# Two buffers for the attention's scaled products, and the mask bounds as a ring of three half blocks

## The chip, the cores and the metric

The kernel runs on one core of a Trainium2 chip. The core has a matrix engine (TensorE, PE in the profile; its weight loads are listed apart as PEld), a vector engine (VectorE, DVE), a scalar engine (ScalarE, ACT), GpSimd (POOL) and SyncE (SP), which here only issues transfers and passes on semaphores. Matmul results go to PSUM, everything else lives in SBUF, and large arrays in HBM. The metric is the device time of one execution in microseconds, the median of several runs.

## The reference

Two graph layers work on x of shape (8, 2048, 256): eight batches of 2048 nodes with 256 features. The mask adj (2048 x 2048, zeros and ones) is common to all batches and to both layers.

```python
# layer 0: attention with 4 heads of 64; keys in 8 chunks of 256, each with a softmax of its own
h = relu(layernorm(x))
q, k, v = h @ Wq.T + bq, h @ Wk.T + bk, h @ Wv.T + bv        # split into heads
scores = clip(einsum('bhnd,bhjcd->bhnjc', q, kc) / 8, -10, 10)
scores = where(mask == 0, -10, scores)
attn = softmax(scores, axis=-1)                              # over the 256 keys of a chunk
ctx = einsum('bhnjc,bhjcd->bhnd', attn, vc)                  # summed over the chunks
out = layernorm(ctx @ Wo.T + bo + h) * gamma + beta
x = x + out
# layer 1: additive graph attention
h = relu(layernorm(x)); g = h @ W
e = leaky_relu(g @ a1 [:, :, None] + g @ a2 [:, None, :], 0.01)
e = where(adj == 0, -1e9, e)
x = x + relu(softmax(e) @ g)
```

Since every chunk has its own softmax, the context of a query is the sum over eight chunks of (exponentials times values) divided by that chunk's sum of exponentials.

## The kernel before

**The mask.** In the setup the mask is turned into *bounds*: one int8 per (key, query), large where the edge exists and -10 times the scale where it does not. A clip of the logits to the bounds (L530, VectorE) then does both the masking and the upper clip; layer 1 uses the same bounds with a comparison (L946, VectorE) that zeroes the weights of missing edges. The bounds of one block of 512 queries against all 2048 keys are 1 MB. There are four such blocks, kept in HBM as `bound_d`, and two of them fit in SBUF at a time (`bound_tile`, tag `bound`, two buffers). They are made from the adjacency in 32 parts, a part being 128 queries by half of the keys: VectorE compares (L277), GpSimd permutes half of the parts (L281), TensorE turns the part (L292), and ScalarE writes the bounds (L303), for the first two blocks straight into the SBUF tiles, for the other two into a small tile `bound_part` that GpSimd's queue (later ScalarE's) sends to HBM (L306). `store_bounds` sends the first two blocks to HBM at slot 2 of the first batch.

**Layer 0, per batch.** Attention runs in 32 steps n = (nb, j): four query blocks nb by eight key chunks j. The steps are software pipelined by hand. Iteration f has a first part `begin` and a second part `end`; at iteration f, step f-1 has its logits and clips, step f-2 its exponentials, its sums and half of its value products, step f-3 the other half of its value products and its scaling. Iteration f stands for the *slots* 2f and 2f+1, and a table `todo` hangs the other work of the batch (norms, output projection, loads, fetches) on slots. The order of instructions on every engine is the order in which the Python code issues them.

In a step TensorE makes the logits (L490), multiplies exponentials and values (L506, into two PSUM tiles `ps_n`) and sums the exponentials with ones (L518, from `both`, which GpSimd adds up in L545). These matmuls use quarters of the array, and a bank of PSUM is written by two of them in turn; a `fence` (L462), which is an empty instruction on SyncE's queue, keeps the two apart. SyncE's queue therefore carries transfers and fences in one order. ScalarE inverts the sums (L550, L551), VectorE multiplies the two `ps_n` by them (`scale`, L560), into `ctxT` for the first chunk of a block, and into a tile `prod` (one buffer) for the other seven. GpSimd's queue then adds prod to ctxT by an accumulating transfer (`gather`, L565). A later scaling writes prod again, so it waits until that transfer has landed. Value products of later steps need the `ps_n` tiles that the scaling frees.

**Layer 1, per batch.** 16 pieces (nb, j4), each of 512 queries by 512 keys. `weights` makes the masked weights on VectorE (L940, L946) two pieces ahead of `products` on TensorE (L963). A whole block of bounds serves four pieces, and a half block two. Meanwhile the batch after the next is loaded and normed (`far`), and the attention of the next batch is begun (`early`).

**When the bounds are fetched** (`fetch_bounds`, L174, SyncE's queue): attention's blocks 1, 2 and 3 at the slots 6 (not in the first batch), 20 and 36; layer 1's block 0 at slot 52 and block 1 at slot 66; layer 1's blocks 2 and 3 and the next batch's block 0 in layer 1's pieces 4, 8 and 12.

Of the kernel before, what the change touches and what calls it, by code (L numbers as in the profile page):

```python
# [8 lines left out]
F32 = mybir.dt.float32  # L9
BF16 = mybir.dt.bfloat16  # L10
I32 = mybir.dt.int32
I8 = mybir.dt.int8
AF = mybir.ActivationFunctionType
ALU = mybir.AluOpType
# [3 lines left out]
P = 128  # L18
# [10 lines left out]
def gnn_two_layers(  # L29
# [18 lines left out]
    nc = tc.nc  # L48
# [5 lines left out]
    NT = N // P  # L54
    NB = 512
    TB = NB // P
    NNB = N // NB
    NCH = N // CHUNK
    KT = CHUNK // P
# [4 lines left out]
    xpool = ctx.enter_context(tc.tile_pool(name="xpool", bufs=2))  # L64
# [29 lines left out]
    work = ctx.enter_context(tc.tile_pool(name="work", bufs=2, reuse_waits="tile"))  # L94
# [20 lines left out]
    bound_d = [kept.tile([P, NT, NB], I8, name=f"bound_d{nb}") for nb in range(NNB)]  # L115
    bounds, bounds1 = {}, {}
# [50 lines left out]
        return queries.rearrange("p (t i b) -> p t i b", i=QUADS, b=Q)  # L167

    def bound_tile():
        return xpool.tile([P, NT, NB], I8, tag="bound", name="bound", bufs=2)  # L170

    def fetch_bounds(nb):
        t = bound_tile()
        nc.sync.dma_start(t, bound_d[nb])  # L174
        return t

    def store_bounds(nb):
        nc.sync.dma_start(bound_d[nb], bounds[nb])


    lone = const.tile([P, NT], F32, name="lone")
# [32 lines left out]
    def pe(piece):  # L214

        piece.kind = "pe"
        return piece
# [40 lines left out]
    def load_rows(t, half):  # L258
        rows = xpool.tile([P, HALF], I32, tag="x", name="rows", bufs=NNB)
        of_block = adj[t // TB * NB:(t // TB + 1) * NB, half * HALF:(half + 1) * HALF]  # L260
        nc.sync.dma_start(rows, of_block.rearrange("(p t) k -> p t k", t=TB)[:, t % TB, :])
        return rows
# [32 lines left out]
    def keep_bounds(pt, t, half):  # L295

        nb, rows, cols = t // TB, slice(half * 8, (half + 1) * 8), slice((t % TB) * P, (t % TB + 1) * P)
        if nb in bounds:
            dst = bounds[nb][:, rows, cols]
        else:  # L300
            tag = part_tags[(2 * t + half) % 4] if in_setup[0] else "r"
            dst = work.tile([P, 8, P], I8, tag=tag, name="bound_part", bufs=2 if tag == "r" else 1)
        nc.scalar.activation(dst, pt, AF.Copy, scale=-2.0 * CLIP * SC, bias=CLIP * SC)  # L303
        if nb not in bounds:
            queue = nc.gpsimd if in_setup[0] else nc.scalar
            queue.dma_start(bound_d[nb][:, rows, cols], dst)  # L306

# [71 lines left out]
    class Projection:  # L379
# [40 lines left out]
        def fetch(self, nb):  # L420
            self.hT[nb] = Features(turned_d[0][nb])
# [47 lines left out]
    class Attention:  # L469
# [55 lines left out]
        def clip(self, n, o):  # L525
            nb, j = self.STEPS[n]
            p, i = self.ORDER[o]
            if (n, p) not in self.e:
                self.e[n, p] = work.tile([P, 2 * KT, NB], F32, tag="e", name="e", bufs=5)
            nc.vector.scalar_tensor_tensor(  # L530
                self.e[n, p][:, i * KT:(i + 1) * KT, :], self.s.pop((n, o)), -CLIP * SC,
                bounds[nb][:, j * KT:(j + 1) * KT, :], op0=ALU.max, op1=ALU.min,
            )

        def exponentials(self, n, o):
# [17 lines left out]
        def scale(self, n, c):  # L553
            nb, j = self.STEPS[n]
            if j == 0 and c == 0:
                self.ctxT[nb] = work.tile([P, 2, NB], F32, tag="ctx", name="ctxT")
            if j > 0 and c == 0:
                self.prod[n] = work.tile([P, 2, NB], F32, tag="prod", name="prod", bufs=1)
            dst = self.ctxT[nb] if j == 0 else self.prod[n]
            nc.vector.tensor_tensor(dst[:, c, :], self.num.pop((n, c)), self.rz[n], op=ALU.mult)  # L560

# [317 lines left out]
    class Layer1:  # L879
# [56 lines left out]
        def weights(self, nb, j4):  # L936
            w = work.tile([P, 4, NB], F32, tag="e", name="w", bufs=5)
            for i in range(4):
                j = 4 * j4 + i
                nc.vector.tensor_scalar(  # L940
                    w[:, i, :], self.src[nb], self.cd[:, 0, j:j + 1], self.cd[:, 1, j:j + 1],
                    op0=ALU.mult, op1=ALU.max,
                )
                if i % 2:
                    two = w[:, i - 1:i + 1, :]
                    nc.vector.scalar_tensor_tensor(  # L946
                        two, bounds1[nb][:, j - 1:j + 1, :], 0.0, two, op0=ALU.is_gt, op1=ALU.mult
                    )
            return w

# [49 lines left out]
    STEPS2 = 2 * STEPS  # L1000
    HALVES = STEPS2 + 6
    PER = STEPS2 // NNB
# [14 lines left out]
    rows = {i: load_rows(*nearest[i]) for i in range(4)}  # L1017
# [20 lines left out]
        for i in parts:  # L1038
            keep_bounds(turn_missing(found.pop(i)), *nearest[i])

    for nb in range(2):
        bounds[nb] = bound_tile()
    proj.stats(1, range(TB))
    proj.power(1)
    proj.shift(1)
# [1 line left out]
    for nb in range(NNB - 1):  # L1047
        i = 6 * nb
# [44 lines left out]
    def layer1_vector(i):  # L1093
# [9 lines left out]

    once = {
        1: [lambda: raws.update(o=load_output_weight(wo)), layer1_weight],
        2: [lambda: store_bounds(0), lambda: store_bounds(1)],
        5: [pe(lambda: turn_weight(raws["o"], woT))],
        6: [lambda: layer1_vector(0)],
        7: [lambda: layer1_vector(1)],
# [8 lines left out]
    for b in range(B):  # L1118
# [4 lines left out]
        ahead = projs.get(b + 1)  # L1123
# [5 lines left out]
        def at(n, *pieces):  # L1129
            todo.setdefault(n, []).extend(pieces)  # L1130
# [4 lines left out]
        def early(i):  # L1135
            one.products(accs[0], ws.pop(i), i)

        def fetch(of, nb):
            of[nb] = fetch_bounds(nb)

        for nb in range(NNB - 1):
            for n, pieces in blocks[nb].beside().items():
# [1 line left out]
        if b == 0:  # L1144
            for n, pieces in once.items():
                at(n, *pieces)

            beats = [(12, 13, 18, 19), (31, 32, 33, 34), (44, 46, 47, 48), (57, 58, 59, 60)]
            for nb, ns in enumerate(beats):
                at(ns[0] - 5, lambda nb=nb: ahead.load(nb))  # L1150
                for t, n in enumerate(ns):
                    at(n, lambda nb=nb, t=t: ahead.stats(nb, [t]))
                n = ns[-1]
                at(n + 1, lambda nb=nb: ahead.power(nb))
                at(n + 2, lambda nb=nb: ahead.shift(nb))
                at(n + 3, lambda nb=nb: ahead.norm(nb, 0))
                at(n + 4, lambda nb=nb: ahead.norm(nb, 1))
                at(n + 4, lambda nb=nb: ahead.flip(nb, 0))
                at(n + 5, lambda nb=nb: ahead.flip(nb, 1))
                at(n + 7, lambda nb=nb: ahead.send(nb))  # L1160
        else:
            at(6, lambda: fetch(bounds, 1))
        at(PER + 4, lambda: fetch(bounds, 2))
        at(2 * PER + 4, lambda: fetch(bounds, 3))
        at(3 * PER + 4, lambda: fetch(bounds1, 0))
        at(STEPS2 + 2, lambda: fetch(bounds1, 1))
        at(STEPS2 - 6, last.load)
        at(STEPS2, lambda: last.residual(0))

# [98 lines left out]
        else:  # L1268
# [33 lines left out]
            last.power1()  # L1302
            last.shift1()
            weights(2)
            last.norm1(0)
            last.norm1(1)
            early(1)
# [9 lines left out]
            one.send(3)  # L1317
            one.receive(2)
            weights(4)

        far = projs[b + 2] = Projection(b + 2) if b + 2 < B else None
        if far:
            far.adder = nc.gpsimd
        for i, (nb, j4) in enumerate(pieces1):
            if not ahead and i < 3:
                continue
            if i + 2 < len(pieces1):
                weights(i + 2)
            if nb not in accs:
                accs[nb] = one.accumulators(nb)  # L1330
            if j4 == 1 and nb + 1 < NNB:
                one.received(nb + 1)
                if nb + 2 < NNB:
                    one.receive(nb + 2)
            if j4 == 2:
                one.alone(nb)
            one.products(accs[nb], ws.pop(i), j4)
            if j4 == 0 and nb > 0:
                one.finish(nb - 1, accs[nb - 1])
            if j4 == 0 and nb > 0 and nb + 1 < NNB:  # L1340
                fetch(bounds1, nb + 1)
            if ahead and (nb, j4) == (NNB - 1, 0):
                fetch(bounds, 0)
            if j4 == 1 and nb > 0:
                one.store(nb - 1)
            if far and i in (3, 6, 9, 12):
                far.send(i // 3 - 1)
            if far and i in (0, 3, 6, 9):
                far.load(i // 3)
            if far and i in (1, 4, 7, 10):  # L1350
                far.stats(i // 3, range(TB))
                far.power(i // 3)
                far.shift(i // 3)
            if far and i in (2, 5, 8, 11):
                for t2 in range(2):
                    far.norm(i // 3, t2)
                for t2 in range(2):
                    far.flip(i // 3, t2)
            if ahead and i == len(pieces1) - 4:
                att = Attention(ahead)  # L1360
            if ahead and i >= len(pieces1) - 4 and i < len(pieces1) - 1:
                att.early(i - (len(pieces1) - 4))
                if i == len(pieces1) - 2:
                    att.early(3)
# [34 lines left out]
```

## Time and profile before

| | us |
|---|---|
| median of 3 runs | 3558.47 (3555.39 to 3564.36) |
| profiled execution | 3563.89 |
| its span, first to last instruction | 3562.1 |
| TensorE busy | 3527.6 |
| VectorE busy | 2639.0 |
| ScalarE busy | 1947.4 |
| GpSimd busy | 1808.9 |
| first sums of exponentials (L518), end of setup | 88.2 |

The profile lists one execution. A busy time is the union of an engine's instructions; "idle before" is the time in which the engine stood still just ahead of an instruction, and the name behind it is what ended it. The ends of matmuls are modelled, so TensorE's busy share is no measure of its rate; the starts are recorded. The rows of SP and of queues (a q behind the engine) are issues of transfers and waits for semaphores, and are not counted as busy.

### The profile page before, as it was taken

Reading aid. Unit: us, or ns where it says so; the run is one execution under the profiler, and the core shown is the slowest. Engines: PE = TensorE matmul, PEld = TensorE weight load, DVE = VectorE, ACT = ScalarE, POOL = GpSimd, SP = SyncE. Lnnn points to the kernel's source line nnn. Section 1 sums busy time; section 2 is a strip of 40 time slices with the busy share of each in tenths; the row PEclk is TensorE's granted clock in tenths of the full one; section 3 lists DMA queues with packets and bytes.
Section 4 is the critical chain, followed back from the end, with each engine's and each line's share of the span. In section 5 each row is a group of like instructions: output and inputs, shape, how many; then the busy total and the mean of one; then the engine's idle time right before and its main releaser. Section 6 shows DMA issues by size and latency. Waiting matters only on the chain.

```text
span 3562.1 us, 104433 instructions
## 1 busy us (share of the span) xinstructions
PE 3527.6 (99%) x46080; PEld 2183.0 (61%) x46080; DVE 2639.0 (74%) x3979; ACT 1947.4 (55%) x2961; POOL 1808.9 (51%) x1182
## 2 busy tenths in 40 slices
PE   8999999999999999999999999999999999999999
PEld 5455785557755577555775557655586555855568
DVE  7888677867678676786767867678586785757866
ACT  6677426763267633676236762367624766147750
POOL 2688016870278702786037850378404784048731
PEclk9999999999999999999999999999999999999999
DMA  7545423444234441344423444234442434124321
GB/s 234 119 107 134 87 74 85 91 113 91 80 79 85 123 95 60 85 96 109 92 66 85 97 110 91 71 79 91 120 103 55 91 81 118 57 55 91 85 69 48
DMA packets 169111, 329.74 MB, mean 93 GB/s; under 512 B 35664, under 2 KB 97360, under 8 KB 160464
## 3 DMA queue, kind: packets, MB, share of 16 engines
q1 hardware_dynamic: 127696, 203.51, 19.2%
q0 software_dynamic: 32640, 118.50, 18.0%
q8 instruction: 360, 5.90, 0.7%
q10 hardware_dynamic: 8320, 1.05, 0.2%
q14 instruction: 95, 0.78, 0.1%
HBM read 154.14 MB, written 51.43 MB: 58 GB/s over the span
## 4 chain that ended last, share of the span: by engine, by line
PE 97%; DVE 1%; DMA 1%; ACT 1%; issue 0%; POOL 0%; ACTq 0%; DVEq 0%; POOLq 0%; SPq 0%
PE ps_s L490 25%; PE ps_n L506 24%; PE ps_s L963 12%; PE ps_t L518 7%; PE ps_n L963 6%; PE ps_t L963 6%; PE ps_t L714 2%; PE ps_t L434 2%; PE ps_n L434 2%; PE ps_s L434 2%; PE ps_t L814 2%; PE ps_n L814 2%; PE ps_t L448 1%; PE ps_n L448 1%; DVE z L277 0%
## 5 line engine op out<-in xcount | busy, mean ns | idle before, releaser
L530 DVE SCALAR_TENSOR_TENSOR e<-ps_s,bound 128x1024 f32<-128x1024 f32 x1024 | 1224.1, 1220 | 404.0 <-PE ps_s L490 400.6
L545 POOL TENSOR_TENSOR both<-e 128x1024 f32<-128x1024 f32 x512 | 1219.8, 2407 | 571.1 <-PE ps_t L518 355.6
L490 PE MATMUL ps_s<-q,k 64*32 64x512 f32 x16384 | 1431.8, 590 | 1.5 <-DVE e L530 1.4
L539 ACT ACTIVATE e<-e 128x1024 f32<-128x1024 f32 x1024 | 1050.6, 1050 | 481.1 <-DVE e L530 462.7
L506 PE MATMUL ps_n<-e,v 64*32 64x512 f32 x16384 | 1224.9, 591 | 2.4 <-DVE prod L560 2.4
L506 PEld LDWEIGHTS ps_n<-e,v 64*32 64x32 f32 x16384 | 460.9, 107 | 473.1 <-issue 384.1
L490 PEld LDWEIGHTS ps_s<-q,k 64*32 64x32 f32 x16384 | 459.5, 106 | 448.6 <-issue 331.2
L518 PE MATMUL ps_t<-both,ones 64*32 64x512 f32 x4096 | 537.9, 592 | 0.1
L963 PE MATMUL ps_s<-g,w 128*128 128x257 f32 x2048 | 447.8, 380 | 0.0
L963 PEld LDWEIGHTS ps_s<-g,w 128*128 128x128 f32 x2048 | 388.8, 190 | 56.3
L560 DVE TENSOR_TENSOR prod<-ps_n,rz 128x512 f32<-128x512 f32 x448 | 288.5, 686 | 162.8 <-PE ps_n L506 96.1
L986 POOL TENSOR_TENSOR x<-x,r 128x256 f32<-128x256 f32 x124 | 90.7, 745 | 466.2 <-ACT r L984 465.4
L946 DVE SCALAR_TENSOR_TENSOR w<-bound,w 128x1024 f32<-128x1024 int8 x256 | 314.7, 1229 | 8.7
L354 POOL TENSOR_TENSOR krn<-krn,mv 128x4 f32<-128x4 f32 x28 | 6.8, 242 | 575.4 <-DVE w L940 575.4
L963 PE MATMUL ps_n<-g,w 128*128 128x257 f32 x1024 | 292.4, 382 | 0.0
L963 PE MATMUL ps_t<-g,w 128*128 128x257 f32 x1024 | 289.7, 380 | 0.0
L550 ACT ACTIVATE rz<-ps_t 128x512 f32<-128x512 f32 x256 | 152.6, 596 | 229.4 <-PE ps_t L518 201.5
L940 DVE TENSOR_SCALAR w<-src,cd 128x512 f32<-128x512 f32 x512 | 263.1, 556 | 7.0 <-ACT src L921 6.6
L963 PEld LDWEIGHTS ps_n<-g,w 128*128 128x128 f32 x1024 | 192.8, 190 | 44.3 <-issue 17.6
L565 POOL DMA_DIRECT2D ctxT<-prod x224 | 191.0, 853 | 54.1 <-DVE prod L560 46.7
L963 PEld LDWEIGHTS ps_t<-g,w 128*128 128x128 f32 x1024 | 193.8, 189 | 28.2
L551 ACT ACTIVATE rz<-rz 128x512 f32<-128x512 f32 x256 | 161.4, 630 | 8.2
(133 smaller groups left out, 2910.4 us busy)
## 6 DMA issues: line engine op xcount, KB each, us to landing
ctxT<-prod POOLq DMA_DIRECT2D x224, 512.0 KB, 4.9
bound<-bound_d SPq DMA_DIRECT2D x62, 1024.0 KB, 6.2
turned_d<-squares SPq DMA_DIRECT2D x232, 128.0 KB, 2.4
hT<-turned_d SPq DMA_DIRECT2D x58, 512.0 KB, 4.3
rows<-in_adj_dram SPq DMA_DIRECT2D x32, 512.0 KB, 5.3
x<-in_x_dram SPq DMA_DIRECT2D x32, 512.0 KB, 4.9
out_dram<-x SPq DMA_DIRECT2D x31, 512.0 KB, 2.6
xp<-in_x_dram SPq DMA_DIRECT2D x28, 512.0 KB, 4.5
```

What stands on the lines that cost most here:

```text
L434: nc.tensor.matmul(in_key_order(pp) if i == 0 else pp, w[:, di, do * P:(do + 1) * P], h, start=di == 0, stop=di == FC - 1,)
L490: nc.tensor.matmul(self.s[n, o][c * Q:(c + 1) * Q, kt, :], self.k[p][rows, at:at + Q], self.q[p][rows, nb * NB:(nb + 1) * NB], start=True, ...
L506: made.append(nc.tensor.matmul(self.num[n, c][h * Q:(h + 1) * Q, :], self.v[rows, j * KT + kt, at:at + Q], self.e[n, p][rows, i * KT + kt, :],
L518: nc.tensor.matmul(self.total[n][h * Q:(h + 1) * Q, :], ones[rows, :], self.both[n, h // 2][rows, h % 2, :], start=half == 1, stop=half == 0,)
L530: nc.vector.scalar_tensor_tensor(self.e[n, p][:, i * KT:(i + 1) * KT, :], self.s.pop((n, o)), -CLIP * SC, bounds[nb][:, j * KT:(j + 1) * K ...
L539: nc.scalar.activation(e, e, AF.Exp, scale=1.0 / SC)
L545: nc.gpsimd.tensor_tensor(self.both[n, p], e[:, 0], e[:, 1], op=ALU.add)
L560: nc.vector.tensor_tensor(dst[:, c, :], self.num.pop((n, c)), self.rz[n], op=ALU.mult)
L565: nc.gpsimd.dma_start(self.ctxT[nb], self.prod.pop(n), accum_op=ALU.add)
L940: nc.vector.tensor_scalar(w[:, i, :], self.src[nb], self.cd[:, 0, j:j + 1], self.cd[:, 1, j:j + 1], op0=ALU.mult, op1=ALU.max,)
L946: nc.vector.scalar_tensor_tensor(two, bounds1[nb][:, j - 1:j + 1, :], 0.0, two, op0=ALU.is_gt, op1=ALU.mult)
L963: nc.tensor.matmul(accs[t][:, 0:F + 1], w[:, i, t * P:(t + 1) * P], g[:, j, :], start=j == 0, stop=j == NT - 1,)
```

## The change

Two things change places in SBUF. `prod` gets two buffers of 4 KB per partition instead of one. The bounds get three buffers of half a block (4 KB per partition each) instead of two of a whole block (8 KB each), half a block being 512 queries by 1024 keys, the first or the second eight of sixteen key tiles. The eight halves of the four blocks are numbered k in the order of use; 0 to 7 serve layer 0, 8 to 15 layer 1, 16 and on the next batch. Half k+3 is fetched when half k has been used: in attention at the slots 12, 20, ... 68 (half 6 at slot 40 instead of 36 in the first batch), and in layer 1 at every second piece. In the setup the first three halves are made in SBUF, so that the second halves of the four parts of block 1 now go through `bound_part`, and three stores of half a block take the place of two.

```diff
     def bound_tile():
-        return xpool.tile([P, NT, NB], I8, tag="bound", name="bound", bufs=2)
+        return xpool.tile([P, NT // 2, NB], I8, tag="bound", name="bound", bufs=3)
+    def of_half(part):
+        nb, half = part
+        return bound_d[nb][:, half * (NT // 2):(half + 1) * (NT // 2), :]
-    def fetch_bounds(nb):
+    def fetch_bounds(part):
         t = bound_tile()
-        nc.sync.dma_start(t, bound_d[nb])
+        nc.sync.dma_start(t, of_half(part))
         return t
...
-        if nb in bounds:
-            dst = bounds[nb][:, rows, cols]
+        if (nb, half) in bounds:
+            dst = bounds[nb, half][:, :, cols]
         else:
             tag = part_tags[(2 * t + half) % 4] if in_setup[0] else "r"
-            dst = work.tile([P, 8, P], I8, tag=tag, name="bound_part", bufs=2 if tag == "r" else 1)
+            dst = work.tile([P, 8, P], I8, tag=tag, name="bound_part", bufs=1 if tag == "o4" else 2)
...
-                bounds[nb][:, j * KT:(j + 1) * KT, :], op0=ALU.max, op1=ALU.min,
+                bounds[nb, j // 4][:, j % 4 * KT:(j % 4 + 1) * KT, :], op0=ALU.max, op1=ALU.min,
...
-                self.prod[n] = work.tile([P, 2, NB], F32, tag="prod", name="prod", bufs=1)
+                self.prod[n] = work.tile([P, 2, NB], F32, tag="prod", name="prod", bufs=2)
...
-    for nb in range(2):
-        bounds[nb] = bound_tile()
+    HALVES_OF = [(nb, half) for nb in range(NNB) for half in range(2)]
+    for part in HALVES_OF[:3]:
+        bounds[part] = bound_tile()
...
-        2: [lambda: store_bounds(0), lambda: store_bounds(1)],
+        2: [lambda: [store_bounds(part) for part in HALVES_OF[:3]]],
...
-        def fetch(of, nb):
-            of[nb] = fetch_bounds(nb)
+        def fetch(k):
+            of = bounds if k < 8 or k >= 16 else bounds1
+            of[HALVES_OF[k % 8]] = fetch_bounds(HALVES_OF[k % 8])
...
-        else:
-            at(6, lambda: fetch(bounds, 1))
-        at(PER + 4, lambda: fetch(bounds, 2))
-        at(2 * PER + 4, lambda: fetch(bounds, 3))
-        at(3 * PER + 4, lambda: fetch(bounds1, 0))
-        at(STEPS2 + 2, lambda: fetch(bounds1, 1))
+        for k in range(8):
+            at(8 * k + (40 - 24 if b == 0 and k == 3 else 12), lambda k=k: fetch(k + 3))
...
             weights(2)
+            fetch(11)
...
             weights(4)
+            fetch(12)
...
+            if i % 2 == 0 and (ahead or i < 10):
+                fetch(i // 2 + 11)
...
-            if j4 == 0 and nb > 0 and nb + 1 < NNB:
-                fetch(bounds1, nb + 1)
-            if ahead and (nb, j4) == (NNB - 1, 0):
-                fetch(bounds, 0)
```

(The fetches of halves 11 and 12 after `weights(2)` and `weights(4)` are those of the last batch, whose layer 1 has a prologue of its own.)

## The prediction

> **What bounds the kernel now.** I read the page from the top: busy times, the chain that ended last, then the waits of each engine, then a timeline of single steps.
>
> ```profile
> PE 3527.6 (99%) x46080; PEld 2183.0 (61%) x46080; DVE 2639.0 (74%) x3979; ACT 1947.4 (55%) x2961; POOL 1808.9 (51%) x1182
> ...
> PE 97%; DVE 1%; DMA 1%; ACT 1%; issue 0%; POOL 0%; ACTq 0%; DVEq 0%; POOLq 0%; SPq 0%
> ...
> ctxT<-prod POOLq DMA_DIRECT2D x224, 512.0 KB, 4.9
> bound<-bound_d SPq DMA_DIRECT2D x62, 1024.0 KB, 6.2
> ```
>
> TensorE carries 97% of the chain, so work taken from another engine is worth nothing; only stalls of TensorE can be won, and 99% busy hides them, because a matmul that is held back between two others still overlaps the modelled end of the one before. So I looked for who is held up by the two things that the change touches, in the waits of VectorE, of the weight loads and of SyncE's queue:
>
> ```profile
> DVE prod L560 <- DMA ctxT<-prod: 50.1, 66, 2.8
> ...
> PEld ps_n L506 <- DVE prod L560: 65.5, 177, 2.3
> ...
> SPq L174 <- DVE e L530: 10.9, 8, 1.4
> ```
>
> Columns: us in total, times, longest. VectorE waited 66 times for the accumulating transfer to leave the single prod buffer, and the weight loads of the value matmuls waited for VectorE's scaling. The bounds appear only as eight waits of SyncE's own queue. Two steps of the second batch show what such a wait costs TensorE (start, duration, engine, line, and in brackets the idle time before it):
>
> ```profile
> 560.20 0.63 PE L518 MATMUL ps_t<-both,ones 64*32 64x512 f32 x4
> ...
> 564.01 1.29 DVE L560 TENSOR_TENSOR prod<-ps_n,rz 128x512 f32<-128x512 f32 x2 [0.86 <-DMA ctxT<-prod]
> ...
> 564.76 0.15 PEld L506 LDWEIGHTS ps_n<-e,v 64*32 64x32 f32 x8 [0.44 <-DVE prod L560]
> ...
> 566.41 0.88 POOL L565 DMA_DIRECT2D ctxT<-prod  x1
> ...
> 568.26 0.63 PE L518 MATMUL ps_t<-both,ones 64*32 64x512 f32 x4
> ...
> 571.16 1.29 DVE L560 TENSOR_TENSOR prod<-ps_n,rz 128x512 f32<-128x512 f32 x2
> ...
> 576.01 0.61 PE L518 MATMUL ps_t<-both,ones 64*32 64x512 f32 x4
> ```
>
> The sums of exponentials (L518) open each step. From 560.20 to 568.26 is 8.06 us, with a wait of 0.86; from 568.26 to 576.01 is 7.75, without one. The gather issued at 566.41 must have landed by 571.1 if the next scaling is not to wait: 4.7 us, while its median landing is 4.9. The deadline sits in the middle of the landing times.
>
> **What the Trainium skill says.** "Perfetto Trace Analysis", section Identifying the Most-Contended Engine, warns that matmul busy share does not tell the distance to the limit; this trace agrees (99% busy, yet steps of 8.06 beside 7.75). Its section Optimization Strategy takes a bubble that repeats as a sign of too few buffers; here it is the prod buffer. "DMA: Bandwidth & Descriptors", section Anatomy of one DMA — SWDGE (gpsimd) path, gives 2.0 us plus bytes over 436e3 for a transfer from this queue: 3.2 us for 512 KB, an estimate; the trace has 4.9, and that is used. The same page, section Two DMAs through the same engine are not ordered, wants the issuing engine to wait for the first transfer before it issues a dependent one. So gathers into one ctxT must still follow each other, on GpSimd's queue now; the trace before shows no such wait, since VectorE's came first.
>
> **The change part by part.**
>
> Second prod buffer. I took from the trace the time between the openings of successive steps and compared each step with the same step of the other batches. The least is 7.725 us for an ordinary step. The excess over the least, over all steps, is 34.8 us. 88 steps have a scaling held by a gather (the 66 of the row above, others that the profile labels with ACT e L539 although the semaphore before it was the transfer's, and less the last two steps of a batch, where other work decides): VectorE idles 52.4 us in them, and their excess is 17.5 us. The two fit: where a step is lengthened, the excess is the wait less 0.52 us (0.86 gives 0.34 above), and all waits under 0.54 cost nothing; 52 steps lie above. With two buffers a scaling waits for the gather two steps back, 4.7 + 7.7 = 12.4 us after its issue; the longest landing is 8.7 us. All these waits go: **-17.5 us**. The other half of the excess (12 us of it in the first batch, whose adjacency pieces add TensorE and VectorE work, and a late hT in the fifth) stays.
>
> Where the lateness goes: to GpSimd's queue, whose next gather must wait for the landing. Between a landing and the next issue the trace has at least 1.7 us (192 pairs); GpSimd's two additions and one issue take 4.73 + 0.85 of 7.7 us. Behind a held gather stands the next addition, and behind that the sums on TensorE. Nothing at the median, 1 us for the one 8.7 us landing, inside GpSimd's 2.1 us of room. Bound 0 to +1; I take 0.
>
> Bounds in halves. 62 fetches of 1 MB become 125 of 512 KB; bytes stay. 63 more issues at 0.34 us are 21 us on SyncE, which waits 1711.9 us for TensorE at the fences (L462). This cover matters, since a fence releases the sums: a fetch that holds the queue holds TensorE. Each of the eight fetches in a batch's attention stands two steps after the step that last reads the buffer it takes, as the old ones at slots 20, 36 and 52 did; those never waited. The eight waits of 10.9 us are the old fetch at slot 66, one slot behind its last reader; it moves to slot 68 and that wait goes, worth nothing, since TensorE's step there was the same. An issue fits between the two fences of a step, some 4 us apart. 0; if the cover were gone, up to +21.
>
> Layer 1's ring. The half that serves the pieces 6 and 7 takes the buffer of pieces 0 and 1. In the second batch VectorE finishes piece 1's weights at 849.95 and starts piece 6's at 873.42; a landing took 4.7 to 9.1 us at twice the size, so some 14 us are spare, and TensorE needs piece 6 only at 850.2 + 6 x 6.94 = 892. The xp load and the src row behind it on SyncE move from 846 to about 850; the xp landing moves by the same 3 to 4 us, into a VectorE lead over TensorE of more than 10 us. 0. The first half for the next batch is issued three pieces, 21 us, before its first clip, two pieces earlier than now.
>
> Setup. Four more parts go through bound_part and GpSimd's queue: 4 x 0.9 us. GpSimd's copies (L281) had idle gaps of 7.4, 1.9, 2.2 and 7.3 us exactly there, so each issue fits; ScalarE's eviction lasts 1.0 us either way. What could suffer is the adjacency row 17, which landed 0.14 us before its comparison began: 128 KB more, in 32 packets of 352 ns over 16 engines, is 0.7 us, and VectorE has 0.46 and 1.66 us of idle time behind it. Bound 0 to +1; I take 0. Three stores of 512 KB instead of two of 1 MB at slot 2: 0.
>
> The order of TensorE's and VectorE's instructions is unchanged. Sum: 3563.9 (the profiled execution, span 3562.1) - 17.5 = **3546.4**. That execution is 5.4 us above the median of 3558.47. If the surplus is the profiler's and the same afterwards, the median goes to 3541.0; if it is itself made of late gathers, the floor is the same 3546.4 and the gain at the median 12.0. I take the middle, **3544 us**, 0.41% faster.
>
> **The rivals.**
>
> Less to win without the profile. The three runs spread from 3555.4 to 3564.4, as they would if the late gathers differ from run to run. Measured from the fastest, the floor of 3546.4 leaves 8.9 us, 0.25%: within 0.3%, about what a measurement of this kernel can tell from no change. For it: landing times crowd around the deadline, so a shift of 0.3 us in them changes the sum by several us. Against: from the median it is still 12.0. Time 3548 to 3552.
>
> The wait moves to GpSimd instead of going. Fetches, x loads (slots 12 and 13, 28 and 29, 44 and 45) now fall in one step with a gather; if these gathers landed later than 7.7 us, each would hold the additions. For it: the slots are neighbours. Against: gathers beside a bound fetch had a median landing of 5.0 against 4.9 without, and only 2 of 224 took over 7 us. If it took back half, 3553.
>
> SyncE's queue becomes the bound: slower. One mechanism: a fetch held by its last reader stands ahead of a fence. 64 such fetches; to lose 10.7 us net of the 17.5 won, each must hold TensorE 0.44 us, that is, wait until about 0.4 us after the fence was due, a whole step later than the clips show. At 1 us each: 3546 + 64 = 3610. Against: no old fetch two steps behind its reader waited at all.
>
> That the second buffer does not take effect is excluded by the landings (8.7 against 12.4 us).
>
> **How the numbers follow.** Forecast (3538 to 3547.7) 0.68; less to win 0.18; moved to GpSimd 0.08; SyncE 0.06. Faster by over 0.3% is below 3547.8: 0.68. Within: 0.18 + 0.08 = 0.26. Slower: 0.06. The range must reach into the second case and leaves out the slow one and the tails: 3538 (17.5 won from the median, and 3 us for a quiet run) to 3554.
>
> **What would show it.** Right: the row of prod waiting for ctxT nearly gone from VectorE's waits; steps of 7.725 us in the batches after the first, whose attention shortens by 1 to 4 us each; GpSimd's gather not waiting for a DMA; the bounds' SyncE waits for L530 gone in attention; first L518 within 1 us of 88.2 us. Wrong: VectorE or GpSimd waiting for DMAs in the same steps, L518's loads waiting longer for the fence than their 0.17 us, clips waiting for a bound DMA, or a first step later than 89 us.

## The result, and the profile after

The kernel after takes 3545.65 us (median of 5 runs, 3543.91 to 3546.29), against 3558.47 us before (3555.39 to 3564.36 over 5 runs). The ratio is 0.9961, 95% interval 0.9947 to 0.9975: 12.8 us, or 0.36%, at the medians. The forecast was 3544 us, range 3538 to 3554, with a chance of 0.68 for faster by over 0.3%: the ratio says 0.39%, with an interval from 0.25% to 0.53%, so this comparison alone doesn't make 0.3% certain. Besides the median, the spread shrank, from 9.0 to 2.4 us. The profiled execution took 3546.29 us (span 3544.5), 17.6 us less than the one before (3563.89, span 3562.1).

From the page of the kernel after: busy times, the chain that ended last by engine, and the two transfers concerned (size, median us from issue to landing).

```profile
PE 3510.8 (99%) x46080; PEld 2273.2 (64%) x46080; DVE 2640.8 (75%) x3979; ACT 1945.5 (55%) x2961; POOL 1810.9 (51%) x1186
...
PE 97%; DVE 1%; DMA 1%; ACT 1%; issue 0%; POOL 0%; ACTq 0%; DVEq 0%; POOLq 0%; SPq 0%
...
ctxT<-prod POOLq DMA_DIRECT2D x224, 512.0 KB, 5.0
bound<-bound_d SPq DMA_DIRECT2D x125, 512.0 KB, 4.6
```

The page looks the same as before: TensorE 99% busy and 97% of the chain, the gather landing in 5.0 us, no faster than its 4.9. What changed is in the waits (us in total, times, longest):

```profile
DVE prod L564 <- PE ps_n L510: 56.8, 116, 11.4
...
PEld ps_t L522 <- SPq L466: 47.2, 248, 1.0
...
PEld ps_n L510 <- DVE prod L564: 42.5, 175, 1.8
```

The row of prod waiting for ctxT (66 times, 50.1 us before) is gone. VectorE's scaling waits for the matmuls that it reads, as it should, and the weight loads' wait for the scaling fell from 65.5 to 42.5 us. The fences (L466, 47.2 us after 49.2) have become no later. Three steps of the second batch in the timeline (start, duration, engine, line):

```profile
560.80 0.61 PE L522 MATMUL ps_t<-both,ones 64*32 64x512 f32 x4
...
565.03 1.29 DVE L564 TENSOR_TENSOR prod<-ps_n,rz 128x512 f32<-128x512 f32 x2
...
568.07 0.83 POOL L569 DMA_DIRECT2D ctxT<-prod  x1
568.52 0.61 PE L522 MATMUL ps_t<-both,ones 64*32 64x512 f32 x4
...
572.76 1.29 DVE L564 TENSOR_TENSOR prod<-ps_n,rz 128x512 f32<-128x512 f32 x2
...
576.25 0.61 PE L522 MATMUL ps_t<-both,ones 64*32 64x512 f32 x4
```

Steps of 7.72 and 7.73 us, and no idle time in brackets behind the scalings. The scaling of 572.76 starts 4.69 us after the issue of 568.07, at the moment that was the deadline before; now nothing of it depends on that transfer.

**Where the 17.6 us came from.** I compared the starts of the steps (first L518, after it L522) one by one. The first 30 steps of each batch's attention became shorter, in us and in the order of the batches, by

```
measured            0.0   1.13  3.71  2.77  2.65  0.94  3.16  1.99   sum 16.35
gather-held, before 0.32  1.38  3.80  2.88  2.75  1.03  3.23  2.07   sum 17.46
```

The second row is the prediction's 17.5 us, batch by batch. The rest nearly cancels: from step 30 to the next batch's first step the time changed by +1.93 and -1.27 (a late hT at the passage to layer 1, in batch 0 after, in batch 4 before; batches counted from 0) and by +1.08 in the five others together; setup +0.16; and the end of the last batch, from its step 30 on, -3.2. That last item was in no part of the prediction and is followed up below.

The second new thing is on SyncE. Its own waits in the kernel after:

```profile
SPq L178 <- DVE w L950: 222.6, 48, 12.0
...
SPq L178 <- DVE stats L347: 102.2, 24, 8.9
```

The eight waits of the bounds for attention's clips (10.9 us) are gone, and 72 waits with 324.8 us stand in layer 1 instead, where before there were 10 with 31.5 us. They hold what stands behind them on the queue and cost nothing: from the first weighted product of layer 1 (L963, after it L967) to the next batch's first sums it is 120.87 us before and after, in every batch.

### The profile page after: what moved, and what is told of

It is laid out like the page before. It is cut to its first block, busy times and chain, and to the rows that moved or that the text cites. A ratio compares the mean times of both kernels' runs of the same rounds, so it can differ in the third digit from the quotient of the medians.

```text
span 3544.5 us, 104574 instructions
## 1 busy us (share of the span) xinstructions
PE 3510.8 (99%) x46080; PEld 2273.2 (64%) x46080; DVE 2640.8 (75%) x3979; ACT 1945.5 (55%) x2961; POOL 1810.9 (51%) x1186
## 4 chain that ended last, share of the span: by engine, by line
PE 97%; DVE 1%; DMA 1%; ACT 1%; issue 0%; POOL 0%; ACTq 0%; DVEq 0%; POOLq 0%; SPq 0%
PE ps_s L494 25%; PE ps_n L510 24%; PE ps_s L967 13%; PE ps_t L522 7%; PE ps_n L967 6%; PE ps_t L967 6%; PE ps_t L718 2%; PE ps_n L438 2%; PE ps_t L438 2%; PE ps_t L818 2%; PE ps_s L438 2%; PE ps_n L818 2%; PE ps_t L452 2%; PE ps_n L452 2%; DVE z L281 0%
## 5 line engine op out<-in xcount | busy, mean ns | idle before, releaser
L494 PE MATMUL ps_s<-q,k 64*32 64x512 f32 x16384 | 1320.4, 590 | 1.6 <-DVE e L534 1.4
L510 PE MATMUL ps_n<-e,v 64*32 64x512 f32 x16384 | 1107.6, 589 | 0.9 <-DVE prod L564 0.9
L494 PEld LDWEIGHTS ps_s<-q,k 64*32 64x32 f32 x16384 | 488.1, 106 | 418.4 <-issue 296.1
L510 PEld LDWEIGHTS ps_n<-e,v 64*32 64x32 f32 x16384 | 507.5, 107 | 380.1 <-issue 280.5
L522 PE MATMUL ps_t<-both,ones 64*32 64x512 f32 x4096 | 544.5, 590 | 0.1
L967 PE MATMUL ps_s<-g,w 128*128 128x257 f32 x2048 | 448.6, 380 | 0.0
L967 PEld LDWEIGHTS ps_s<-g,w 128*128 128x128 f32 x2048 | 389.4, 190 | 56.5
L564 DVE TENSOR_TENSOR prod<-ps_n,rz 128x512 f32<-128x512 f32 x448 | 289.0, 688 | 138.7 <-ACT rz L555 65.5
L967 PE MATMUL ps_n<-g,w 128*128 128x257 f32 x1024 | 292.4, 382 | 0.0
L967 PE MATMUL ps_t<-g,w 128*128 128x257 f32 x1024 | 289.8, 380 | 0.0
L522 PEld LDWEIGHTS ps_t<-both,ones 64*32 64x32 f32 x4096 | 150.2, 106 | 112.2 <-issue 49.7
L967 PEld LDWEIGHTS ps_n<-g,w 128*128 128x128 f32 x1024 | 192.8, 190 | 44.3 <-issue 17.6
L967 PEld LDWEIGHTS ps_t<-g,w 128*128 128x128 f32 x1024 | 193.8, 189 | 28.2
```

The costliest lines, as they stand in the source:

```text
L494: nc.tensor.matmul(self.s[n, o][c * Q:(c + 1) * Q, kt, :], self.k[p][rows, at:at + Q], self.q[p][rows, nb * NB:(nb + 1) * NB], start=True, ...
L510: made.append(nc.tensor.matmul(self.num[n, c][h * Q:(h + 1) * Q, :], self.v[rows, j * KT + kt, at:at + Q], self.e[n, p][rows, i * KT + kt, :],
L522: nc.tensor.matmul(self.total[n][h * Q:(h + 1) * Q, :], ones[rows, :], self.both[n, h // 2][rows, h % 2, :], start=half == 1, stop=half == 0,)
L967: nc.tensor.matmul(accs[t][:, 0:F + 1], w[:, i, t * P:(t + 1) * P], g[:, j, :], start=j == 0, stop=j == NT - 1,)
```

## The experiments

My theory: with one prod buffer a gather that lands later than about 4.7 us after its issue holds VectorE's scaling, then the value matmuls; the whole gain is that wait. Rivals: that the ring of small fetches brings part of the gain (shorter landings, a freer SyncE); that the lateness is only handed to GpSimd's queue; that SyncE's fetches hold the fences. A kernel with two prod buffers and whole blocks of bounds isn't among the runs; it would take 4 KB per partition more than either kernel. Each ratio is against the kernel before on the same chip in the same session; its medians there were 3559.35, 3562.19, 3561.73 and 3561.00 us for the four groups.

### The ring without the second buffer, and a fetch moved alone

The kernel after with the second buffer taken back (small setup tiles that share prod's place, `bound_part`, go back to one buffer with it), and the kernel before with one number changed:

```diff
-                self.prod[n] = work.tile([P, 2, NB], F32, tag="prod", name="prod", bufs=2)
+                self.prod[n] = work.tile([P, 2, NB], F32, tag="prod", name="prod", bufs=1)
...
-            dst = work.tile([P, 8, P], I8, tag=tag, name="bound_part", bufs=1 if tag == "o4" else 2)
+            dst = work.tile([P, 8, P], I8, tag=tag, name="bound_part", bufs=2 if tag == "r" else 1)
```

> The kernel after with the second prod buffer taken back; the ring of half blocks stays. Theory (the gain is the scaling's wait for the gather): the row of prod waiting for ctxT returns to VectorE's waits with 60 to 75 entries and 45 to 60 us, and with it the 12 us at the median; only the 3 us that the last batch's step 30 won may stay, because they are put down to the fetch that moved from slot 66 to slot 68. Median 3554 to 3558. Rival (smaller, evenly spread fetches shorten the gathers' landings and bring part of the gain): the row has under 40 entries, median below 3551.

```diff
-        at(STEPS2 + 2, lambda: fetch(bounds1, 1))
+        at(STEPS2 + 4, lambda: fetch(bounds1, 1))
```

> The kernel before with one line changed: the fetch of layer 1's second block goes from slot 66 to slot 68, two steps behind its last reader. Theory A (SyncE held by this fetch is what lets TensorE stand 1.4 us and then run at half rate at the end of the last batch): the eight SyncE waits for the clip of 10.9 us go, the idle time near the last batch's step 30 falls below 1 us, no slow stretch after it, and the time falls by about 3 us, to 3555. Theory B (the late gather there is the cause): the waits go and the time stays at 3558 within its spread.

Measured: ring alone 3559.24 us, ratio 0.9995 (0.9986 to 1.0003); fetch later 3560.47 us, 1.0001 (0.9993 to 1.0010). The ring by itself is worth nothing that shows, and its spread is the wide one again (3552.8 to 3562.9). Its 57 waits and 3559.24 us lie just outside the expected 60 to 75 and 3554 to 3558, far from the rival's under 40 and below 3551; the 3 us that the expectation kept for the moved fetch didn't stay. VectorE's and the weight loads' waits with the ring alone:

```profile
PEld ps_n L510 <- DVE prod L564: 62.1, 174, 2.4
...
DVE prod L564 <- DMA ctxT<-prod: 46.5, 57, 2.5
```

The wait is back, so it is the second buffer that removes it. Moving the fetch took SyncE's eight waits for L530 away and brought no time that shows, as theory B and the prediction had it. It also left TensorE's idle time near the last batch's step 30 at 1.89 us, and the ring alone had 1.48 there: this idle time belongs to the late gather, since both kernels have the fetch at slot 68; with two buffers it is 0.87, and still 0.87 where the fetch goes back to slot 66 (below). What follows the idle time differs. Two stretches of the kernel before and one of the kernel with the later fetch (window, its length, busy us of each engine with instructions; then the granted TensorE clock, the DMA share and GB/s):

```profile
3406.00:3410.00 4.00, 2.56 (x42) 0.73 (x38) 1.56 (x3) 3.16 (x5) 3.94 (x2) 1.00 0.98 269
3410.00:3417.50 7.50, 7.40 (x68) 1.89 (x56) 0.00 (x0) 0.89 (x2) 4.06 (x4) 0.54 0.63 168
```

```profile
3408.40:3416.00 7.60, 7.13 (x84) 2.59 (x85) 1.74 (x3) 2.87 (x7) 4.61 (x4) 1.00 0.68 181
```

In the profiled execution of the kernel before the clock was at half speed for 6.8 us after 1.44 us of idle time (0.54 is the mean of the 7.5 us shown); in the other one it stayed at 1.00 after 1.89 us. From the last batch's step 30 to the end it is 158.5 us in the kernel before, 155.9 with the later fetch, 155.5 with the ring alone and 155.3 after. So most of the 3.2 us at the end of the last batch was a throttle that this one execution met, not something the fetch does.

### A shorter landing instead of a buffer

The kernel before, one buffer, whole blocks:

```diff
-                nc.gpsimd.dma_start(self.ctxT[nb], self.prod.pop(n), accum_op=ALU.add)
+                nc.gpsimd.dma_start(self.ctxT[nb][:, 0:1, :], self.prod.pop(n)[:, 0:1, :], accum_op=ALU.add)
```

> The kernel before, with one prod buffer and whole blocks, but each gather adds only the first 64 of the context's rows per head pair (256 KB of 512), so the second half of the accumulated context is left out. Theory (a landing of 4.9 us against a deadline of 4.7): the landing falls to about 4 us or less and meets the deadline; the row of prod waiting for ctxT goes from 66 entries to under 15, and the time falls by 10 to 13 us, to 3545 to 3549, without any second buffer. Rival (the wait is a matter of the buffer's release and not of the landing's length, or the landing is not set by bytes): over 40 entries, time 3555 to 3559.

Measured: 3546.63 us, ratio 0.9963 (0.9951 to 0.9975), spread 3546.1 to 3549.3. Its transfer row:

```profile
ctxT<-prod POOLq DMA_DIRECT2D x224, 256.0 KB, 3.3
```

and its waits of the scaling, where no row for ctxT is left:

```profile
DVE prod L560 <- PE ps_n L506: 127.5, 157, 11.4
```

A landing of 3.3 us meets the deadline and gives the whole gain, and the narrow spread, with one buffer and without the ring. The rival, that the landing's length doesn't matter, is out. Half the bytes also ease other transfers (the bounds land in 5.1 us where they took 6.2), so the next experiment moves the issue and leaves the bytes.

### The issue moved later, with one buffer and with two

Memsets of a small new tile on GpSimd delay each gather; the same edit in the kernel before and the kernel after:

```diff
+                for _ in range(8):          # 8, 1 or 2 memsets
+                    nc.gpsimd.memset(pad, 0.0)
                 nc.gpsimd.dma_start(self.ctxT[nb], self.prod.pop(n), accum_op=ALU.add)
```

> The kernel before with eight small memsets on GpSimd ahead of each gather, which issue it some 0.5 to 0.8 us later. Theory (the deadline of 4.7 us sits in the middle of the landing times): nearly every gather is late now; summing what 224 landings of the kernel before exceed the deadline by gives, scaled to the 17.5 us of the unshifted sum, 25 to 45 us more, so 3583 to 3604, and the row of prod waiting for ctxT has over 150 entries. Rival (TensorE has room for later gathers, the waits only coincide with long steps): under 10 us more.

> The kernel after, with the same eight memsets ahead of each gather. Theory (with two buffers the deadline is 12.4 us after the issue, and GpSimd has 2.1 us of room in a step): no waits for the gather and the time within 2 us of the kernel after, 3544 to 3548. Rival (the lateness has moved to GpSimd's queue, and the additions with the sums behind them are at their limit): the additions come late and the time is 10 us or more above, 3556 and up.

> The kernel before with one memset (0.13 us, and 0.38 us until the transfer behind it is issued) ahead of each gather, where eight took 1.7 us. Theory (deadline in the middle of the landings): of the 224 landings of the kernel before nearly all miss a deadline that is 0.5 us earlier; the sum of what they exceed it by, less 0.52 each, rises by 53 us, and half to all of that shows: 3585 to 3615. Rival (only GpSimd's own time counts, as for eight memsets with two buffers): 0 to 5 us more, 3560 to 3567.

> The kernel after with one memset ahead of each gather. Theory (two buffers remove the gather's deadline, and GpSimd has room for 0.5 us in a step, though not for the 1.7 us of eight memsets): 0 to 4 us more, 3545 to 3550, no waits of VectorE for the gather. Rival (GpSimd has no room at all behind the second buffer): 0.5 us in each of 224 steps, some 3600 and up.

> The kernel before with two memsets ahead of each gather, some 0.5 to 0.65 us (one had moved the issue by under 0.1, eight by 1.6). Theory (deadline in the middle of the landings): the sum over the 224 landings of what they exceed the deadline by, less 0.52 each, rises by 4 to 8 us for 0.05 to 0.1 us of delay (4.7 measured with one memset), by about 300 for 1.6 (323 measured with eight), and by 53 to 77 for 0.5 to 0.65: 3613 to 3640. Rival (up to some delay TensorE has room, and the 323 us are GpSimd's): under 15 us more, 3577 at most.

> The kernel after with the same two memsets ahead of each gather. Theory (two buffers take the gather's deadline away; the 112 us that eight memsets cost are GpSimd's own queue, which 1.6 us more in a step fill): 0 to 6 us more, 3545 to 3552. Rival (the lateness only moved to GpSimd): as much as with one buffer, or at least 0.3 us in each of 224 steps, 3610 and up.

The delay is read from the traces as the median time from the end of the addition to the issue, less the same in the kernel before or after: 1.67 us for eight memsets, 0.04 for one (the issue doesn't wait for it), 0.66 for two. "By the landings" is the rise of the sum, over the 224 landings of the kernel before, of what they exceed 4.7 us less the delay by, less 0.52 each.

| memsets, delay | by the landings | one buffer | two buffers |
|---|---|---|---|
| 1, 0.04 us | +3 us | 3566.47, ratio 1.0022 (1.0011 to 1.0033) | 3550.04, ratio 0.9966 (0.9954 to 0.9978) |
| 2, 0.66 us | +79 us | 3617.96, ratio 1.0162 (1.0147 to 1.0177) | 3556.88, ratio 0.9990 (0.9982 to 0.9999) |
| 8, 1.67 us | +303 us | 3885.67, ratio 1.0908 (1.0892 to 1.0925) | 3657.52, ratio 1.0270 (1.0255 to 1.0285) |

With one buffer the medians rise by 4.7, 57.0 and 323.5 us: hardly at first, and then steeply. Two memsets are the clean test: in the first 30 steps of the batches, where the clock stays at full speed, the profiled execution is 58 us longer than that of the kernel before, for the 79 read from the landings, and the median of 3617.96 us lies within the expected 3613 to 3640. That is what a deadline in the middle of the landings does. Both expectations for eight memsets missed, their delay of 1.67 us being well over the assumed 0.5 to 0.8; a single memset with one buffer missed its own and ended where its rival had it (3560 to 3567), since the delay was 0.04 and not 0.5, so it decides little.

The timeline of the kernel with one buffer and two memsets:

```profile
558.09 0.75 PE L519 MATMUL ps_t<-both,ones 64*32 64x512 f32 x4
...
558.77 0.86 POOL L568 DMA_DIRECT2D ctxT<-prod  x1 [0.39 <-issue]
...
564.01 1.29 DVE L561 TENSOR_TENSOR prod<-ps_n,rz 128x512 f32<-128x512 f32 x2 [1.69 <-DMA ctxT<-prod]
564.75 0.15 PEld L507 LDWEIGHTS ps_n<-e,v 64*32 64x32 f32 x8 [1.25 <-DVE prod L561]
...
567.09 0.61 PE L519 MATMUL ps_t<-both,ones 64*32 64x512 f32 x4
```

A landing of 5.2 us, a scaling 1.69 us late, loads 1.25 us late, a step of 9.00 us.

That 323.5 comes close to 303 is partly chance, for eight memsets with one buffer bring in a second cause. Mean clock of the execution, and VectorE's wait for the gather:

```profile
core 0: 3878.2 us, clock 0.975
...
DVE prod L561 <- DMA ctxT<-prod: 308.6, 107, 7.0
```

The clock was at half speed for 198 us, in 40 stretches (17 us in 4 stretches before, mean clock 0.998). In the first 30 steps of the eight batches the excess over the least step is 345 us; 227 of them are in the 59 of 240 steps that such a stretch touches, and the other steps have a median excess of 0.15. The waits were fewer than expected (107, not over 150) and longer, because some landings grew too: a tenth took over 7.6 us, where it was 5.7 before. Late gathers, long landings and the falls of the clock behind the long waits are not told apart in this run.

With two buffers the same 0.66 us cost 11.2 us against the kernel after (by the ratios, 0.9990 less 0.9961, 10.3), over the expected 0 to 6. A single memset ended at the upper edge of its forecast (3550.04 for 3545 to 3550), and eight cost some 112 us, as the rival of that expectation had it (3556 and up). VectorE waits for no gather in any of them. The loss is on GpSimd's queue. With two memsets 6.2 of the 9.7 us lost in the first 30 steps sit in the steps 17, 18 and 26 of the batches (counted from 0; step 18: 8.06 us for 7.74; step 26: 8.06 for 7.72). They stand behind the steps 16 and 24, where GpSimd has two pieces of other work (L770, L742) besides the gather. The timeline of that kernel, from a step with one such piece into step 16:

```profile
652.25 4.73 POOL L550 TENSOR_TENSOR both<-e 128x1024 f32<-128x1024 f32 x2 [0.18 <-PE ps_t L523]
...
665.32 0.87 POOL L572 DMA_DIRECT2D ctxT<-prod  x1 [0.39 <-issue]
665.92 1.58 POOL L770 TENSOR_TENSOR x<-x,o 128x512 f32<-128x512 f32 x1
667.17 1.57 POOL L742 TENSOR_TENSOR hn<-hn,bo_r 128x512 f32<-128x512 f32 x1
668.41 5.01 POOL L550 TENSOR_TENSOR both<-e 128x1024 f32<-128x1024 f32 x2
```

With one piece GpSimd still stands idle for 0.18 us (0.86 in the kernel after) and the step keeps its length. With two it has no idle time left, so the additions (`both`) and the sums behind them come late. In the kernel after GpSimd is already busy for 7.72 of 7.72 us there. In the kernel with eight memsets and two buffers over half of the steps are lengthened (121 of the 210 in batches 1 to 7 by more than 0.1 us), and the sums wait for GpSimd (loads of L523, us in total, times, longest):

```profile
PEld ps_t L523 <- POOL pad L571: 71.8, 108, 2.2
...
POOL ctxT L572 <- DMA ctxT<-prod: 35.8, 26, 4.4
```

The second line is the wait that a second buffer hands to GpSimd, gathers of one ctxT waiting for each other. So the second rival is right once the gathers come late enough. With two memsets it occurs once (2.4 us), and in the kernel after not at all: the closest landing there came 0.71 us before the next issue, where it was 1.71 before.

### Fetches closer behind their readers

The kernel after with the last fetch, then all of them, put one step closer behind their readers:

```diff
-            at(8 * k + (40 - 24 if b == 0 and k == 3 else 12), lambda k=k: fetch(k + 3))
+            at(8 * k + (40 - 24 if b == 0 and k == 3 else 10), lambda k=k: fetch(k + 3))   # only k == 7 in the first run
```

> The kernel after with only the last of the attention's eight fetches put back from slot 68 to slot 66, one slot behind its reader. Theory (a hold of SyncE of some 1.4 us costs TensorE nothing in an ordinary batch): eight SyncE waits for a clip of about 11 us return, time within 1 us of the kernel after, 3545 to 3547. If the hold alone starts the slow stretch at the end of the last batch: 3548 to 3549. If each hold costs TensorE its length: 3556.

> The kernel after with all of the attention's fetches one step earlier (10 + 8k instead of 12 + 8k, the one exception of the first batch left), so that each stands one step closer behind its last reader and holds SyncE's queue until that clip has ended. Theory (a hold of 1.4 us ahead of a fence is hidden in TensorE's step): over 50 SyncE waits for the clip, 70 us or more of them, and the time within 4 us of the kernel after, 3545 to 3550. Rival (SyncE's queue becomes the bound, 1 us for each hold): 3590 to 3610.

Measured: 3546.10 us, ratio 0.9961 (0.9949 to 0.9973), with 8 waits of 12.4 us; and 3548.27 us, ratio 0.9959 (0.9945 to 0.9973), with this row in SyncE's waits:

```profile
SPq L178 <- DVE e L534: 102.5, 62, 2.2
```

62 holds of 1.65 us each ahead of the fences cost nothing that shows: both ratios are those of the kernel after. The slow rival is out by a wide margin.

### Three small transfers moved

The late hT is left in the traces of both kernels. At the seven passages to layer 1 its fetch lands after 3.7 to 12.2 us in the kernel after (median of all hT fetches 4.2), and two sends of 2 KB in single elements are issued 0.4 and 0.9 us behind it. To see whether these slow it, and to gain on both kernels, the kernel after with

```diff
             last.fetch1()
-            one.send(1)
-            one.send(2)
             ahead.values(2)
-            one.receive(1)
...
             last.ends(1)
+            one.send(1)
+            one.send(2)
+            one.receive(1)
             one.total()
```

> The kernel after with the three small transfers of layer 1's source terms (two sends of 2 KB in single elements and the receive behind them) moved on SyncE's queue from behind the fetch of the last block's hT to behind the values that read it. Theory (the sends' packets slow that fetch from 4 us to 10 to 12 us, and TensorE at times waits 1 to 2 us for it): hT lands in about 4 us in every batch, the wait of L818 for it goes, and the time falls by 1 to 3 us, to 3543 to 3545. Rival (the source terms now come late and hold ScalarE and the next pieces): 3547 and up.

Measured: 3549.60 us, ratio 0.9968 (0.9956 to 0.9979): no gain, and in the range of the rival (3547 and up). But nothing that waits stands between the old place and the new on SyncE's queue, so the sends were still issued 0.4 and 0.9 us behind the fetch, and hT landed after 3.8 to 12.5 us as before. So this is no test of either: whether the sends delay hT stays open.

## Why the prediction was right, step by step

- **TensorE bounds, and 99% busy hides stalls.** Right. Both pages show 99%; the 16.35 us are visible only in the steps.
- **The second prod buffer, -17.5 us.** Right in mechanism and size: -16.35 in the first 30 steps of the eight batches, each batch within 0.35 us of its own share. The deadline of 4.7 us within the landings is borne out by the half gather and by two memsets (58 us for 79 forecast); the 0.52 us of slack was tested only as a part of that sum.
- **The other half of the excess stays.** Right: the first batch's 30 steps, with most of it, took the same time after (0.0 us of change); the late hT moved from the fifth batch to the first.
- **Lateness goes to GpSimd, 0.** Right for this change: no gather waited for a landing. Its term "2.1 us of room" was too large: that is the room of a step without other work on GpSimd. Step 16 of the kernel after has none, and a delay of 0.66 us already costs 11 us.
- **Bounds in halves on SyncE, 0, up to +21.** Right, and shown directly: the ring alone 0.9995, and 62 holds of 1.65 us without a loss that shows. That the wait at slot 66 was worth nothing is the later fetch's 1.0001.
- **Layer 1's ring, 0.** Right in time. The text's shift of 3 to 4 us for the loads behind a fetch was too small: the fetches hold SyncE up to 12.0 us.
- **Setup, 0.** Right: first sums at 88.4 us, after 88.2.
- **Sum against median.** The sum for the profiled execution was 3546.4, measured 3546.29. The choice that failed was the middle between "the surplus of 5.4 us is the profiler's" (3541.0) and "it is late gathers" (3546.4). It was late gathers: the profiled execution after is 0.6 us above its median, and the spread goes where the waits go, with the second buffer and with the half gather alike. 3544 was 1.65 us low for that. That the sum came out to 0.1 us is part luck: the end of the last batch gave 3.2 us that nothing in the prediction foresaw, and the late hT and the edges of the attention took most of it back.
- **The rivals.** "Less to win without the profile" had the right view of the surplus but measured from the fastest run; the medians differ by 12.8. "The wait moves to GpSimd" didn't happen in the kernel after: the gathers waited for no landing. It was nearer than the prediction had it, since 0.66 us of delay take back most of the gain (0.9990). "SyncE becomes the bound" didn't come near.

## What to carry to other kernels

When a buffer comes free through a transfer, compare the time from issue to next use with the whole distribution of landings, not with the median: a deadline inside it costs a little in many steps, and here it showed as a spread from run to run as well. A shorter transfer (0.9963) and one more buffer (0.9961) were then worth the same, and the gain could be summed beforehand, step by step. When a delay is put in as a test, keep it small and read the granted clock: a large one can bring a slower clock with it. Before trusting the engine that inherits the wait, take its room in its fullest step, not in an ordinary one.

## What the hardware showed that was not expected

- An accumulating transfer from GpSimd's queue landed in 4.9 us for 512 KB and 3.3 us for 256 KB, medians of 224 each. The Trainium skill's page "DMA: Bandwidth & Descriptors", section Anatomy of one DMA — SWDGE (gpsimd) path, gives 3.2 and 2.6 us, an estimate: the trace's 1.6 us for the second 256 KB is well over the page's 0.6, and the measurement decides.
- TensorE's granted clock fell to half speed for 6.8 us after an idle time of 1.44 us in one execution, and stayed at 1.00 after 1.48 and 1.89 us at the same place in two others. "TensorE: Matmul & The Clock Gate", section HAM oscillation — how this bites in real kernels, speaks of idle times over some 3.4 us; this trace had one of less than half. The section What's actually happening adds that the window in which activity is watched runs freely. The traces agree: within each of them all falls of the clock lie within 6 ns of one grid of 3.413 us. In the kernel with eight memsets and one buffer, from 100 us on, the 36 windows of this grid ahead of a fall had TensorE busy for at most 0.48 of the window, and all others at full clock for at least 0.51. In the kernel before the window ahead of the fall had 0.58, and one of 0.57 in the ring alone had no fall behind it, so these busy shares, whose ends are modelled, don't settle where the line is.
- A gather issued behind one memset on GpSimd was hardly delayed (0.04 us); behind two it waited 0.39 us beyond their 0.27.
